# Last attention and expert choice of an eight-phase model: units of two heads and of one head in turn, experts chosen sequence by sequence

## The chip, the core and the metric

The kernel runs on one core of a Trainium2 chip. Its time is the device time in microseconds (us) of one execution. Five engines work side by side, each through its own queue in order: PE (matrix products and transposes), DVE (vector work), ACT (functions such as exp, and copies), POOL (vector work on SBUF, and the indirect DMAs) and SP (which only issues DMAs). They wait for each other through semaphores. "us" is microseconds throughout, and L12 is line 12 of the kernel before unless the text says "after".

## The reference, cut to what matters

Eight sequences of 256 tokens and 256 features pass through four layers; each layer is an attention and a feed-forward block, each followed by a residual and a layer norm. The change touches the last attention and the last block.

```
# last attention, per half sequence of 256 rows (16 heads of width 16, 4 key heads)
scores = softmax(energy / sqrt(D))                # two maps per head, a = 0 and 1
diff   = softmax(where(causal, NEG, scores[0] - lam * scores[1]))
att    = einsum(diff, v); att = att * rsqrt(mean(att * att)) * rms_w * (1 - LAM_INIT)
x      = layernorm(x + att @ Wo)

# last block: 32 experts, the best 4 of each token
p      = softmax(x @ gate)
w, idx = top_k(p, 4); w = w / w.sum()
y[t]   = sum_k w[t, k] * ((u * silu(g)) @ down[idx[t, k]]),   g, u = split(x[t] @ gate_up[idx[t, k]])
x      = layernorm(x + y)
```

The kernel takes whole sequences of 256 tokens, so an attention has 8 sequences, two query blocks of 128 rows each (`qc` 0 and 1; block 0 sees 128 keys, block 1 sees 256) and 16 heads, held as 4 stripes of 32 partitions times 4 heads.

## The kernel before, in words

**Attention, `attn3`.** A *unit* is a query block `qc` and `nh = 2 - qc` heads of each stripe, so that a unit always holds 512 score columns in each of four PSUM banks: two heads with 128 keys, or one head with 256. A sequence has six units. Before the change they run in the order (qc 0, head 0), (qc 0, head 2), then qc 1 with heads 0, 1, 2, 3. The order of all work is written out by hand (a manual schedule for the four compute engines; SP's DMAs are placed by the framework). The loop over `n` (48 units and 3 more turns) does in each turn:

- for the unit before: `factors` (a reciprocal on DVE L671; causal masks L676 and two small products L681, L682 on POOL);
- one step of the queue `others`;
- for unit n: `scores` (32 or 16 matmuls L641, four mask matmuls L654, four maxima on DVE L658, 16 or 8 exponentials on ACT L661);
- for unit n-3: `values` (L738), and a copy of the finished output;
- one step of `projections` (the next sequence's q, k and v: 13 steps, most of them a product L595 and a DVE multiply L599), the first half of `differences` for the unit before (DVE L695 and the maximum L699; POOL L700 and the scaling L703), one or two more steps of `projections` (two when unit n has qc 0);
- one step of `ends` (the finish of an earlier sequence: transposes L755, root mean square, output product L803, residual L164, layer norm, transposes L154; six steps);
- the second half of `differences`;
- two more steps of `others`, unless `self.scattering` is set;
- for unit n-2: `turned` (transposes L720, exponential L722).

DVE, PE, ACT and POOL each carry out their share of that list in exactly this order. The transposes, projections, finish and sort share the PSUM tag `t` with two buffers.

**Sort, `ffn3_sort`, `place`, `tile_experts`, `scatter`.** The tokens are handled in two groups of four sequences (`GROUPS`). For a group the sort computes all gate logits of its eight 128-row pieces (L1906, 32 matmuls with their passes), subtracts the maximum and takes the exponential (L1911 to L1916), finds the best eight and their indices for each piece (L1921, L1922), compares with an iota into one-hot rows (L879), counts and ranks them with matmuls (L893), adds up counts (L896, L898), places every expert at a multiple of 128 rows (L907 to L914), reads out each token's four slots (L921, L922, L926), scatters the rows of X to `rows` in DRAM with 32 indirect DMAs on POOL (L953), finds the expert of each 128-row tile (L935 to L944), and normalises the four weights (L1934 to L1936). It is a generator: the `yield`s cut it in steps. Group 0's sort is put into `others` when sequence 3 is finished, with three scatters a step (`each=3`).

**Experts, `ffn3`, `ffn3_experts`, `ffn3_combine`.** For each group 63 tiles of 128 rows are fetched three at a time (`xg`, L1959, on SP), transposed (L1970, L1972), multiplied by their expert's weights (L1978), passed through silu and a product (L1985, L1987; a one-element POOL copy L1990 follows), transposed back (L1994, L1996), multiplied by the down weights (L2000, L2008) 8 tiles later (4 in group 1) and stored (L2010). The down weights are loaded after the first two fetches, when the attention's buffers come free. During group 0's tiles, `left` is stepped: while more than one generator is left, only at every third tile; it holds the finish of the last sequence, then group 1's sort. During group 1's tiles the outputs of group 0 are gathered (L2045, 32 indirect DMAs on POOL), weighted and normed; group 1's follow at the end.

Of the kernel before, what the change touches and what calls it, by code (L numbers as in the profile page):

```python
# [10 lines left out]
F32 = mybir.dt.float32  # L11
BF16 = mybir.dt.bfloat16  # L12
I32 = mybir.dt.int32
# [26 lines left out]
class Model:  # L40


    def __init__(self, ctx, tc, ins, out):
        self.tc, self.nc, self.ins, self.out = tc, tc.nc, ins, out
        nc = self.nc
        self.const = ctx.enter_context(tc.tile_pool(name="const", bufs=1, side="left"))
        self.small = ctx.enter_context(tc.tile_pool(name="small", bufs=4, side="left"))
        self.psum = ctx.enter_context(
            tc.tile_pool(name="psum", bufs=2, space=bass.MemoryType.PSUM)
        )  # L50
        self.n_ev = 0
        self.rows, self.outs = (
            [
                nc.dram_tensor(f"{x}{g}", (n * P, D), F32, kind="Internal").ap()
                for g, n in enumerate(TILES)
            ]
            for x in ("rows", "outs")
        )
        self.lrows, self.louts = (
            [  # L60
                nc.dram_tensor(f"{x}{g}", (n * P, d), F32, kind="Internal").ap()
                for g, n in enumerate(TILES0)
            ]
            for x, d in (("lrows", ROW0), ("louts", P))
        )
        self.left = []
        self.scattering = False
        self.sorted, self.sorted0 = {}, {}

        c = self.const  # L70
        self.X = [c.tile([P, 2, D], F32, name=f"X{b}", tag=f"X{b}") for b in range(NB)]
        self.xT = [c.tile([P, 2, BLK], F32, name=f"xT{k}", tag=f"xT{k}") for k in range(NBLK)]
        self.ident = c.tile([P, P], F32, name="ident")
        nc.sync.dma_start(out=self.ident, in_=ins["c_ident"])
        self.load_x(0, 2)

        self.tri = c.tile([P, 2 * P], F32, name="tri")
        self.identb = c.tile([P, P], BF16, name="identb")
        nc.vector.tensor_copy(self.identb, self.ident)
        self.maskA = c.tile([P, 4, P], BF16, name="maskA")  # L80
        self.one32 = c.tile([P, 32], F32, name="one32")
        nc.vector.memset(self.one32, 1.0)
        self.nhalf = c.tile([P, 16], F32, name="nhalf")
        nc.gpsimd.memset(self.nhalf, -0.5)
# [25 lines left out]
    def after(self, *call):  # L110

        self.left.append(call)

    def copy(self, out, in_):

# [436 lines left out]
    def attn3(self, w, act, keep, start=False, beside=None):  # L552
# [2 lines left out]

        nc = self.nc
        lam_init = 0.8 - 0.6 * math.exp(-0.3 * 0)

# [187 lines left out]
        def finish(b):  # L748
# [61 lines left out]
            self.normed(b, r, *m)  # L810
            yield
            self.norm_done(b, last=False)
            if beside and b == GROUPS[0][1] - 1:
                others.append(beside(keep))
            yield

        others = []
        projections, ends, done = [], [], []

        def step(queue, n=1):  # L820

            while n and queue:
                if next(queue[0], StopIteration) is StopIteration:
                    queue.pop(0)
                else:
                    n -= 1

        for _ in project(0):
            pass
        units = [  # L830
            Unit(b, qc, h0) for b in range(NB) for qc in range(2) for h0 in range(0, 4, 2 - qc)
        ]
        for n in range(len(units) + 3):

            def at(back):
# [6 lines left out]
                    projections.append(project(u.b + 1))  # L842
            if last:
                last.factors()
            step(others)
            if u:
                u.scores()
            if at(3):
# [5 lines left out]
            step(ends)  # L854
            next(halves, None)
            next(halves, None)
            if not self.scattering:
                step(others, 2)
            if at(2):
                at(2).turned()  # L860
            ends += done
            done.clear()
        return ends + others


    def place(self, w, act, keep, name, idx, n, E=32, tag="t"):
# [1025 lines left out]
            gup=self.load(pool, "f3_gup", [P, 32, 2, 192], split=8),  # L1892
        )

    def ffn3_sort(self, w, g, act, each=1):

        nc = self.nc  # L1900
        first, n = GROUPS[g]
        n *= 2
        lg = self.ps("t")[:, : n * 32].rearrange("p (t e) -> p t e", e=32)
        for t in range(n):
            for c in range(2):
                nc.tensor.matmul(  # L1906
                    lg[:, t, :], self.xt(first + t // 2, t % 2, c), w["gate"][:, c, :],
                    start=(c == 0), stop=(c == 1),
                )
        nm = act.tile([P, n], F32, tag="r_nm", name="r_nm", bufs=1)  # L1910
        nc.vector.tensor_reduce(nm, lg, AX.X, ALU.max)  # L1911
        pr = act.tile([P, n, 32], F32, tag="r_pr", name="r_pr", bufs=1)
        nc.vector.tensor_tensor(
            pr, lg, nm.unsqueeze(2).to_broadcast([P, n, 32]), ALU.subtract
        )
        nc.scalar.activation(pr, pr, AF.Exp)  # L1916
        yield
        top = act.tile([P, n, 8], F32, tag="r_top", name="r_top", bufs=1)
        idx = act.tile([P, n, 8], U32, tag="r_idx", name="r_idx", bufs=1)
        for t in range(n):  # L1920
            nc.vector.max(top[:, t, :], pr[:, t, :])  # L1921
            nc.vector.max_index(idx[:, t, :], top[:, t, :], pr[:, t, :])  # L1922
            if t % 4 == 3 or t == n - 1:
                yield
        one, slots, ends = yield from self.place(w, act, self.const, f"f3{g}", idx[:, :, 0:4], n)
        rows = self.scatter(
            self.rows[g], slots, lambda t, k: self.X[first + t // 2][:, t % 2, :]
        )
        next(rows)
        expert = yield from self.tile_experts(w, act, self.const, f"f3{g}", ends)  # L1930

        wt = self.const.tile([P, n, 4], F32, tag=f"r_w{g}", name="r_w", bufs=1)
        sm = act.tile([P, n], F32, tag="r_sm", name="r_sm", bufs=1)
        nc.vector.tensor_reduce(sm, top[:, :, 0:4], AX.X, ALU.add)  # L1934
        nc.vector.reciprocal(sm, sm)
        nc.vector.tensor_tensor(  # L1936
            wt, top[:, :, 0:4], sm.unsqueeze(2).to_broadcast([P, n, 4]), ALU.mult
        )
        self.sorted[g] = wt, slots, expert
        self.scattering = True  # L1940
        yield
        for i, _ in enumerate(rows):
            if i % each == each - 1:
                yield
        self.scattering = False

    def ffn3_experts(self, w, g, act):


        nc = self.nc  # L1950
        rows, outs, expert, tiles = self.rows[g], self.outs[g], self.sorted[g][2], TILES[g]
        xg, xT, h, hT, er = {}, {}, {}, {}, {}

        def fetch(j):
# [71 lines left out]
                    f(j - i)  # L2026
            yield

    def ffn3_combine(self, g, act, ahead):


        nc = self.nc
        first, n = GROUPS[g]
        wt, slots, _ = self.sorted[g]
        ys, rs = {}, {}
        for t in range(2 * n + ahead):
            i = t - ahead
# [22 lines left out]
                self.norm_done(b)  # L2060
                yield

    def ffn3(self, w, act, left, start=False):

        self.down = None
        if start:
            for b in range(NB):
                self.transpose_x(b)  # L2070
            left = [self.ffn3_sort(w, 0, act)]
        if 0 not in self.sorted:
            for x in left:
                for _ in x:
                    pass
            left = []
        left = list(left) + [self.ffn3_sort(w, 1, act)]
        for j, _ in enumerate(self.ffn3_experts(w, 0, act)):

            if len(left) > 1 and j % 3 != 2:  # L2080
                continue
            while left and next(left[0], StopIteration) is StopIteration:
                left.pop(0)
        for x in left:
            for _ in x:
                pass
        put = self.ffn3_combine(0, act, 2)
        for j, _ in enumerate(self.ffn3_experts(w, 1, act)):

            if j >= 8:  # L2090
                next(put, None)
        for _ in put:
            pass
        for _ in self.ffn3_combine(1, act, 1):
            pass


# [1 line left out]
def tile_layers(ctx: ExitStack, tc: tile.TileContext, ins, out, phases):  # L2099
# [26 lines left out]
    for i, name in enumerate(phases):  # L2126
        m.last = i == len(phases) - 1
        with tc.tile_pool(name=f"act{i}", bufs=2, side=sides[i % 2]) as act:
# [4 lines left out]
            with tc.manual_schedule(engines=engines) if name in MANUAL else ExitStack():  # L2133
# [13 lines left out]
                elif name == "attn1":  # L2147

                    def then(i=i):
                        keeps[i - 1].close()  # L2150
                        open_weights(i + 1)

                    m.attn1(w, act, left, then, start=start)
                elif name == "attn3":
                    beside = None
                    if not m.last:
                        beside = partial(m.ffn3_sort, stack[i + 1][1], 0, each=3)
                    left = m.attn3(w, act, kept[i], start=start, beside=beside)
                elif name == "ffn3":
                    m.ffn3(w, act, left, start=start)  # L2160
                    keeps[i - 1].close()
                else:
                    getattr(m, name)(w, act, start=start)
        stack[i][0].close()
# [125 lines left out]
```

## Time and profile before

| what | us |
|---|---|
| median of 5 runs (lowest to highest) | 2531.3 (2523.01 to 2536.96) |
| the profiled execution | 2531.85 |
| its span in the profile | 2530.1 |
| last attention: first L658 to last L738 | 1767.2 to 2223.9 |
| experts of group 0: first L1970 to last down product L2000 | 2227.85 to 2364.66 |
| experts of group 1: to the last store's landing | to 2473.0 |
| last gathers and norms: to the end | to 2530.1 |

The page gives busy time, not bound time: an engine may be busy for most of a stretch and still not set its length. So the prediction goes by stretches, by what each engine waited for in them, and by the distance between the same instruction of successive units (for attention: the first of the four maxima L658) or tiles (L1987).

### The profile page before, as it was taken

To read this page: it belongs to the slowest core of one execution; us is meant where nothing else is said; L and a number is where in the kernel's file an instruction comes from. 1 tells how busy PE (TensorE), PEld (TensorE's weight loads), DVE (VectorE), ACT (ScalarE), POOL (GpSimd) and SP (SyncE) were. 2 spreads that over 40 slices of the span, in tenths; PEclk is the share of its full clock that TensorE was granted. 3 is DMA by queue.
4 is the path that set the end of the run, shared out by engine and by line. 5 is a ranking of instruction groups with operands and counts; after the bars stand their busy time and mean duration, and the time that the engine had idled before them with its cause. 6 is when DMAs were issued, how large, how long until landed. Compare 5 with 4: busy or idle time off the path is not lost. (4 is left out here: it accounts for less than half of the span.)

```text
span 2530.1 us, 36310 instructions
## 1 busy us (share of the span) xinstructions
PE 2203.4 (87%) x12016; PEld 1493.2 (59%) x12016; DVE 1430.3 (57%) x3593; ACT 1046.9 (41%) x3005; POOL 918.5 (36%) x1725
## 2 busy tenths in 40 slices
PE   7999789899999999999999999998788777678890
PEld 4455588756666666666664465555555554467770
DVE  4555486754544543544465454556888887735363
ACT  1234355553544544544431112221766756634440
POOL 1222443343433323333312320001566657824445
PEclk9999899999999999999999999999989988799995
DMA  5000411100000100000250011002000000155663
GB/s 158 1 1 1 158 46 40 57 9 4 4 3 4 51 1 1 1 1 1 83 195 0 1 50 51 1 1 102 1 2 1 2 1 28 40 144 177 198 195 96
DMA packets 92309, 120.76 MB, mean 48 GB/s; under 512 B 9757, under 2 KB 79582, under 8 KB 91102
## 3 DMA queue, kind: packets, MB, share of 16 engines
q1 hardware_dynamic: 82270, 95.75, 11.7%
q0 software_dynamic: 8192, 21.11, 2.7%
q8 instruction: 100, 1.64, 0.3%
q10 hardware_dynamic: 1664, 1.57, 0.2%
q14 instruction: 83, 0.68, 0.1%
HBM read 67.53 MB, written 50.88 MB: 47 GB/s over the span
## 5 line engine op out<-in xcount | busy, mean ns | idle before, releaser
L1388 POOL TENSOR_SCALAR p<-p,rs 128x128 f32<-128x128 f32 (+1 forms) x256 | 104.8, 429 | 294.4 <-DVE rs L1386 290.1
L1378 ACT ACTIVATE p<-ps_s,nm,rq 128x128 f32<-128x128 f32 (+1 forms) x256 | 128.0, 507 | 151.8 <-DVE nm L1376 151.8
L1306 ACT ACTIVATE sq<-ps_a 128x512 f32<-128x512 f32 x126 | 76.0, 603 | 227.3 <-PE ps_a L1298 225.1
L146 POOL TENSOR_SCALAR rsq<-bnmv 128x2 f32<-128x2 f32 x64 | 13.7, 214 | 383.9 <-DVE bnmv L184 376.3
L661 ACT ACTIVATE e<-ps_a,nm 128x128 f32<-128x128 f32 (+1 forms) x256 | 105.9, 435 | 110.0 <-DVE nm L658 96.4
L1307 DVE TENSOR_REDUCE ssk<-sq 128x4 f32<-128x512 f32 x64 | 43.8, 686 | 172.6 <-ACT sq L1306 172.6
L703 POOL TENSOR_SCALAR v<-e,r,nmd 128x128 f32<-128x128 f32 (+1 forms) x256 | 135.0, 540 | 10.0
L1298 PE MATMUL ps_a<-w_a_wq,xT 128*128 128x512 f32 x256 | 122.3, 600 | 12.1 <-DVE k L1320 9.2
L1978 PE MATMUL ps_a<-w_f_gup,xTg 128*128 x504 | 111.7, 345 | 14.8 <-issue 6.5
L720 PE MATMUL ps_t<-ident,v 128*128 128x128 f32 x384 | 68.2, 314 | 62.1 <-DVE qT L599 30.7
L1298 PE MATMUL ps_a<-w_a_wv,xT 128*128 128x512 f32 x256 | 120.5, 593 | 1.0 <-ACT q L1331 1.0
L695 DVE SCALAR_TENSOR_TENSOR e<-e,c 128x128 f32<-128x128 f32 (+1 forms) x256 | 105.4, 461 | 22.2 <-POOL c L682 22.0
L1307 DVE TENSOR_REDUCE ssq<-sq 128x4 f32<-128x512 f32 x64 | 43.9, 686 | 130.2 <-ACT sq L1306 130.2
L1298 PE MATMUL ps_a<-w_a_wk,xT 128*128 128x512 f32 x248 | 116.5, 593 | 0.0
L1426 PE MATMUL ps_o<-w_a_wo,attT 128*128 128x256 f32 x512 | 111.8, 379 | 0.0
L661 ACT ACTIVATE e<-ps_s,nm 128x128 f32<-128x128 f32 (+1 forms) x256 | 106.8, 452 | 0.0
L1426 PEld LDWEIGHTS ps_o<-w_a_wo,attT 128*128 128x128 f32 x512 | 96.7, 190 | 12.8
L1162 DVE SCALAR_TENSOR_TENSOR yg<-ps_t,xg,yg 128x128 f32<-128x128 f32 x266 | 93.0, 350 | 13.9 <-PE ps_t L1151 3.7
L1365 PE MATMUL ps_s<-kT,qT 128*128 128x256 f32 (+1 forms) x512 | 100.2, 329 | 0.0
L1978 PEld LDWEIGHTS ps_a<-w_f_gup,xTg 128*128 128x128 f32 x504 | 81.8, 196 | 28.6 <-issue 13.8
L720 PEld LDWEIGHTS ps_t<-ident,v 128*128 128x128 f32 x384 | 49.6, 161 | 81.5 <-POOL nmd L700 30.0
L1412 PE MATMUL ps_o<-pT,V 128*128 128x256 f32 x256 | 79.5, 392 | 19.2 <-ACT pT L120 19.2
(410 smaller groups left out, 6067.5 us busy)
## 6 DMA issues: line engine op xcount, KB each, us to landing
rows<-zero SPq DMA_DIRECT2D x42, 384.0 KB
xg<-rows SPq DMA_DIRECT2D x42, 384.0 KB
outs<-yg SPq DMA_DIRECT2D x42, 384.0 KB
w_f_gup<-in_f_gup SPq DMA_DIRECT2D x8, 768.0 KB
w_f_w<-in_f_w SPq DMA_DIRECT2D x8, 512.0 KB
w_f_down<-in_f_down SPq DMA_DIRECT2D x8, 384.0 KB
w_f_up<-in_f_up SPq DMA_DIRECT2D x5, 512.0 KB
lrows<-zero SPq DMA_DIRECT2D x12, 204.0 KB
```

The lines of the kernel that those rows point to most:

```text
L661: nc.scalar.activation(e[:, s, j * nk : (j + 1) * nk], sc[s][:, j, :], AF.Exp, bias=nm[:, s, j : j + 1], scale=1.0, accum_out=sums[:, s, j ...
L695: nc.vector.scalar_tensor_tensor(d[:, s, h, :], u.e[:, s, h, 1, :], u.c[:, s, h : h + 1], d[:, s, h, :], ALU.mult, ALU.add,)
L703: nc.gpsimd.tensor_scalar(u.v[:, s, h, :], d[:, s, h, :], u.r[:, s, h, 0:1], nm[:, s, h : h + 1], ALU.mult, ALU.add,)
L720: nc.tensor.transpose(ps[:, s, c, :], x, self.ident)
L1162: nc.vector.scalar_tensor_tensor(acc[j], y, c, acc[j], ALU.mult, ALU.add)
L1298: nc.tensor.matmul(ps, self.xt(u.b, t, c), w[which][:, c, u.cols], start=(c == 0), stop=(c == 1),)
L1307: nc.vector.tensor_reduce(out, sq, AX.X, ALU.add)
L1365: nc.tensor.matmul(sc[:, j, :], u.qT[:, h0 + j, qc * P : (qc + 1) * P], u.kT[:, h0 + j, 0:nk], start=(j == 0), stop=False,)
L1378: nc.scalar.activation(u.p[qc][:, h0 + j, :], sc[:, j, :], AF.Exp, bias=nm[:, j : j + 1], scale=r[:, j : j + 1], accum_out=u.sums[qc][:, h ...
L1388: nc.gpsimd.tensor_scalar(u.p[qc][:, j, :], u.p[qc][:, j, :], ri[:, j : j + 1], 1.0, ALU.mult, ALU.mult,)
L1426: nc.tensor.matmul(y[:, t, :], attTs[b][:, h, t * P : (t + 1) * P], w["wo"][:, h, :], start=(h == 0), stop=(h == 15),)
L1978: nc.tensor.matmul(ps, xT[j][:, c, :], w["gup"][:, bass.ds(er[j], 1), c, :].rearrange("p o f -> p (o f)"), start=(c == 0), stop=(c == 1),)
```

## The change

Four things change, in `attn3`, `ffn3` and what they call.

- **Order of units.** Within a sequence the units now run (qc 0, head 0), (qc 1, head 0), (qc 1, head 1), (qc 0, head 2), (qc 1, head 2), (qc 1, head 3).
- **Choice by sequence.** `ffn3_sort` is split. `ffn3_choose` does one sequence: logits, a copy out of PSUM, best eight, one-hot rows, counts and ranks; it goes into `others` when that sequence is finished. `ffn3_place` does the rest for a group, once its four sequences are chosen. Sequences 0 to 5 are chosen during the attention; sequence 6 is queued in its last turn and sequence 7 during group 0's tiles, where before all of group 1 was sorted.
- **Scatters have their own queue.** `sends` holds them, two a step for group 0; while it is not empty, the step of `others` ahead of `scores` is a step of `sends`. After the differences `others` has one step, where it had two.
- **The softmax.** The best eight are found on the logits themselves. The exponential of the four best, less the best, and their normalisation are taken per group in `ffn3_weights`: for group 0 ahead of its first tile, for group 1 after its last.

At the start of `ffn3` what is left in `sends` is issued before the first fetch. The core of the diff (`ffn3_place` is the second half of the old sort with other names and other cuts; the counts of a sequence's two pieces are added to those before by one DVE instruction each, and the slots take one more; `step(j)` belongs to `ffn3` and runs once per tile of group 0):

```diff
-            if beside and b == GROUPS[0][1] - 1:
-                others.append(beside(keep))
+            if beside and b < NB - 1:
+                others.append(self.ffn3_choose(beside, keep, b))
+                if b == GROUPS[0][1] - 1:
+                    others.append(self.ffn3_place(beside, 0, keep, sends, each=2))
             yield
...
-            Unit(b, qc, h0) for b in range(NB) for qc in range(2) for h0 in range(0, 4, 2 - qc)
+        order = ((0, 0), (1, 0), (1, 1), (0, 2), (1, 2), (1, 3))
+        units = [Unit(b, qc, h0) for b in range(NB) for qc, h0 in order]
...
-            step(others)
+            step(sends or others)
...
-            if not self.scattering:
-                step(others, 2)
+            step(others)
...
+    def ffn3_choose(self, w, keep, b):
...
+        ps = self.ps("t")[:, :64].rearrange("p (t e) -> p t e", t=2)
+        for t in range(2):
+            for c in range(2):
+                nc.tensor.matmul(ps[:, t, :], self.xt(b, t, c), w["gate"][:, c, :], ...)
+        nc.vector.tensor_copy(lg, ps)
+        yield
+        for t in range(2):
+            nc.vector.max(top[:, t0 + t, :], lg[:, t, :])
+            nc.vector.max_index(idx[:, t, :], top[:, t0 + t, :], lg[:, t, :])
+        nc.vector.tensor_copy(fi, idx[:, :, 0:4])
+        nc.vector.tensor_tensor(one[:, two] ..., ALU.is_equal)
+        yield
+        yield
+        for x, m in ((0, self.ones), (1, self.behind)):
+            for k in range(4):
+                nc.tensor.matmul(ps[:, x], m, one[:, two, k, :], ...)
...
+        yield
...
+    def ffn3_weights(self, g, keep):
+        nc.vector.tensor_tensor(wt, top[:, :, 0:4], top[:, :, 0:1].to_broadcast([P, n, 4]), ALU.subtract)
+        nc.scalar.activation(wt, wt, AF.Exp)
+        nc.vector.tensor_reduce(sm, wt, AX.X, ALU.add)
+        nc.vector.reciprocal(sm, sm)
+        nc.vector.tensor_tensor(wt, wt, sm.unsqueeze(2).to_broadcast([P, n, 4]), ALU.mult)
...
+        def step(j):
+            if ends and j % 3 == 2:
+                self.step(ends)
+                if not ends:
+                    others.append(self.ffn3_choose(w, keep, last))
+                    others.append(self.ffn3_place(w, 1, keep, sends))
+            elif others:
+                self.step(others)
+            else:
+                self.step(sends)
+        wt = self.ffn3_weights(0, keep)
+        while sends:
+            self.step(sends)
```

## The prediction

> **What bounds the kernel now.** The change only touches the last fifth, so I read that by stretches: first the busy time of each engine per stretch, then what DVE waited for in the same stretches, then two stretches of the timeline.
>
> ```profile
> core 0: us, PE busy (x) PEld busy (x) DVE busy (x) ACT busy (x) POOL busy (x), PEclk, DMA share, GB/s
> ...
> 1983.00:2037.00 54.00, 43.21 (x362) 29.82 (x362) 45.95 (x103) 38.15 (x151) 33.62 (x82) 0.91 0.00 1
> 2037.00:2092.00 55.00, 39.42 (x256) 27.18 (x256) 45.06 (x129) 26.93 (x99) 25.85 (x62) 0.75 0.00 1
> 2092.00:2146.00 54.00, 40.68 (x329) 27.25 (x329) 44.44 (x103) 31.77 (x128) 41.04 (x81) 0.88 0.09 33
> 2146.00:2200.00 54.00, 38.30 (x308) 24.92 (x308) 38.04 (x85) 35.78 (x145) 46.12 (x92) 0.78 0.11 40
> ...
> 2244.00:2362.00 118.00, 102.58 (x586) 85.35 (x586) 52.21 (x182) 49.68 (x182) 45.24 (x96) 0.97 0.48 156
> ```
>
> The first row is one undisturbed sequence of the attention: DVE is busy 46 of 54 us, more than any other engine, and PE's waits there are for DVE to empty PSUM. The second holds group 0's sort, the next two its scatters: POOL climbs to 41 and 46. The last row is group 0's experts: PE is busy 103 of 118.
>
> The waits of DVE in the plain stretch, in the sort and in the scatters (who waited, for whom, us in total, times, longest):
>
> ```profile
> DVE V L619 <- PE ps_t L615: 2.7, 1, 2.7
> DVE nm L658 <- PE ps_a L654: 1.9, 2, 1.4
> ...
> DVE r_nm L1911 <- PE ps_t L1906: 3.3, 1, 3.3
> DVE r_upto L896 <- PE ps_t L893: 2.4, 1, 2.4
> ...
> DVE e L695 <- POOL c L682: 7.6, 7, 2.9
> DVE nm L658 <- PE ps_a L654: 7.2, 6, 1.9
> ```
>
> So a plain sequence has some 8 us of DVE waits; the sort adds two waits for its own matmuls; while rows are scattered DVE waits for POOL's factor c. How the scatter stands in POOL's queue:
>
> ```profile
> 2159.62 0.42 POOL L676 TENSOR_SCALAR_AFFINE_SELECT e<-e 128x256 f32<-128x256 f32 x1
> 2160.21 1.03 POOL L953 DMA_INDIRECT rows<-X,r_slots  x1 [0.17 <-issue]
> 2161.54 0.97 POOL L953 DMA_INDIRECT rows<-X,r_slots  x1 [0.30 <-issue]
> 2162.82 0.96 POOL L953 DMA_INDIRECT rows<-X,r_slots  x1 [0.30 <-issue]
> 2163.81 0.29 POOL L700 TENSOR_TENSOR nmd<-nmd,r 128x2 f32<-128x2 f32 x1
> ...
> 1932.95 0.20 POOL L700 TENSOR_TENSOR nmd<-nmd,r 128x4 f32<-128x4 f32 x1 [1.47 <-DVE nmd L699]
> ```
>
> Three scatters of 1.28 us stand between the masks and L700, and L700 then starts at once: POOL was late. Without scatters (last line) POOL waits at that place for DVE.
>
> **The change part by part.** The sum is made against the profiled execution, 2531.85 us (span 2530.1 and 1.75 around it); the median of the runs is 2531.3, so a difference holds for both.
>
> *The old sort leaves the attention.* From one unit's first L658 to the next, in the timeline: units 32 to 36, with the sort, took 15.17, 15.61, 13.07, 9.49 and 10.73, together 64.1; the same places a sequence earlier (26 to 30) 9.63, 8.22, 7.06, 9.88 and 10.20, together 45.0. **-19.1**. The sort's own DVE instructions sum to 14.5 in the groups of that stretch: DVE work is paid here nearly one for one, plus 4.6 of waits.
>
> *Six choices come in, per sequence.* DVE, each: copy of 128x64 logits, between L896's 0.19 and the 128x128 copy's 0.29: 0.23; per piece L1921 and L1922 are 0.39 apart from the next: 0.8; cast 0.17; one-hot row of 256 elements 0.42 (L914's size); counts and slot 3 x 0.2. Together 2.25. PE: 8 passes of L1906's 0.11 (3.5 us for 32) and 8 of L893 (0.9 at four times the width). The copy stands behind the second half of the differences, when its matmuls have long been possible; but PE's first maxima of the next unit already come 1.9, 1.5 and 1.4 us late at this place of a sequence (L658's wait of units 15, 21 and 27), and the best-eight instructions, 1.4 us, fill that wait. Against it, the logits hold one of the two buffers of `t`, so that the two transposes of `turned` go one after the other (one exponential of 0.6 between them). Counts and ranks stand ahead of the next scores on PE: 0.3 to 0.9. From below: 1.4 of 2.25 hidden and little of PE's part left, 1.0 each. From above: the two waits of the old sort stay at full size, 3.3 + 2.4 + 2.25 = 7.9 each. The old 3.3 was for 32 passes and the new one for 8 that are issued early, so I go by the DVE work: 2.0 each, **+12** (6 to 47).
>
> *Placement stays*, in smaller steps: L907 to L926 ran from 2081.92 to 2087.5 without a gap, the experts of tiles 1.3: **+6.9** (6 to 8.5). Weights, 0.6, go to the start of the experts, where everything waits for DMA.
>
> *Scatters, two a unit in place of three.* POOL's wait ahead of L700 in a plain sequence (1874 to 1928) was 1.47, 1.74, 3.36, 1.81, 1.48 and 2.32. Three scatters, 3.84, overflow it by 1.8 on average; two, 2.56, by 0.67. Units 37 to 41 took 48.97 against 43.33 for 25 to 29; units 42 to 46 took 44.53 against 43.6, though the projections of a next sequence were missing, 13 x 0.41, of which 4.5 fall to five units. So 11 units paid about 11 for an overflow of 20; 15 units with an overflow of 10 pay 5.5. **-5.5** (-10 to 0).
>
> The clock belongs here. In the scatter stretches TensorE was granted 0.88 and 0.78, in the plain one 0.91, and the sort's row has 0.75. [...] I stay with POOL's count, since the plain row falls below full clock as well.
>
> *Order of units.* Nothing is added or removed: per sequence DVE's sum is the same 46. POOL's longer share of a two-head unit (masks 1.28 against 0.84, scaling 3.5 against 2.2) no longer comes twice running, where DVE waited 0.4 for c (unit 14); but the second one now meets the finish's square roots, where POOL waits 1.95 for ACT's tables, and c was late by 1.2 (unit 17) already. **0** (-5 to +5).
>
> *Start of the experts.* Before, the scatters ended at 2211.2, and the first fetch, waiting for the attention's last buffers, went out at 2224.08; six tiles were done by 2239 and the seventh waited for its rows until 2244.4, behind 3.1 MB of down weights at some 240 GB/s. After the change the last four scatters stand behind POOL's last scaling (2222.1), 5.1 us, and land about 2229.5. SP is in order: two of the eight weight loads go ahead of the fetch, the other six queue behind it. The bytes are the same; the DMA engines lose the gap, about 1.5 to 2, and PE restarts without the 5.7 us pause. **+1.5** (0 to 6).
>
> *Group 0's tiles.* L1987's 21st to 30th starts took 27.3 us, the next 23 1.67 each: the old sort cost 10.6 there (logits 3.5 and two table loads of 1.28 in one tile of 7.12, counts 3.0, the rest under 1 a tile). After the change it is one sequence's choice, no table load, and the same placement: 0.8 + 0.5 + 0.9 + 2.1 = 4.3. **-6.3** (-9 to -2). The last scatter of group 1 comes after the 63rd tile's product in place of the 62nd, and the fetch behind it, with two stores behind that on SP, was the last wait at this boundary (PE idle 3.7 before 2363.9): **+1.4** (0 to 2).
>
> *Group 1's weights* need a table load (1.28) after the last silu. Eight gathers of 1.25 on POOL come first in time: 0; without this cover 2.5.
>
> Sum: -19.1 + 12 + 6.9 - 5.5 + 0 + 1.5 - 6.3 + 1.4 = **-9.1**: 2522.7, given as 2523.
>
> **The rivals.**
>
> *More is hidden.* 8 us of DVE waits per sequence stand open. If the choices fall into them down to the lower end (1.0 each, -6) and the order of units takes 4 with it: -19, **2512.5**. For it: the score waits of units 15, 21 and 27 stand exactly where the best-eight instructions come. Against: the old sort paid more than its DVE work.
>
> *Slower: each choice waits on PE.* Place: the logits' copy and the counts, each an in-order DVE instruction behind a fresh matmul, with the next maxima, the exponentials and the projections queued behind it. Price: half of the old waits, 2.9 and 2.25, 5.2 each. The gain is gone from 3.5 each on; above 4.8 the kernel is slower by more than 0.3%. At 5.2: +19 on the sum, **2542**.
>
> *It does nothing measurable.* If the attention goes by DVE's sum alone, sort and choices together are 6 x 2.25 + 6.9 - 14.5 = +5.9 (in place of -0.2), and if the first tiles wait for the late scatters at the upper end, +6: 5.9 - 5.5 + 6 - 6.3 + 1.4 = +1.5, **2533**. For it: the first row above, and the place of the last scatters. Against: the five long units, which lost more than the sort's own instructions.
>
> **How the numbers follow.** Forecast 0.45, more hidden 0.17, nothing measurable 0.18, slower 0.20. Measurement tells about 0.3%, 7.6 us, from no change: faster is below 2524.3. The forecast's own range is -16 to -2 (2516 to 2530), of which 0.28 is faster, 0.17 the same. Faster 0.28 + 0.17 = 0.45, with 0.01 of the third case 0.46; same 0.17 + 0.17 = 0.34; slower 0.20. The range runs from the second case with the scatters' lower end (-23.5, 2508) to the slower case at its named price, 2542; below and above about 0.1 each.
>
> **What would show it.** The five units with the sort shrink from 64 to about 53; each sequence with a choice grows from 54.4 by about 2; DVE's wait for c falls from 7.6 to about 3 in a stretch of 100 us; no L1911-like wait above 1 us at the choice's copy; the first fetch goes out 4 to 6 us after the last attention product, the seventh tile's rows land about 22 us after it; the 21st to 30th tile products take about 21 us. I am wrong if the choices' DVE waits exceed 1.5 each, if the order of units moves a plain sequence by over 1 us, or if the seventh tile comes later than 26 us after the attention.

## The result and the profile after

The changed kernel takes 2538.0 us (median; 2527.7 to 2541.7) against 2531.5 of the kernel before on the same chips: a ratio of 1.0021, 95% interval 1.0014 to 1.0027. The forecast was 2523 us; the time lies in its range, on the other side of no change and within the 0.3% named there. The profiled execution took 2538.62 us (span 2536.9).

Lines have moved: L658 is now L667 (maxima of the scores), L695 and L699 are L704 and L708, L700 and L703 are L709 and L712, L682 is L691, L720 is L729, L953 is L956. From the first maximum of unit 0 to that of unit 46 the attention took 427.1 us before and 436.5 after. Busy time by stretch after the change, with the columns that the prediction's first fence has: three sequences with a choice each (units 12 to 29), the scatters (units 36 to 45) and group 0's tiles.

```profile
1866.10:2044.10 178.00, 134.79 (x1140) 90.96 (x1139) 141.39 (x342) 111.58 (x439) 101.84 (x246) 0.90 0.00 1
2106.10:2205.60 99.50, 74.11 (x581) 50.70 (x581) 77.24 (x189) 61.16 (x252) 75.45 (x151) 0.81 0.09 30
2244.00:2362.00 118.00, 103.87 (x601) 87.18 (x601) 54.30 (x181) 52.21 (x188) 45.28 (x104) 0.94 0.59 183
```

Units 12 to 29 took 160.7 before with 136.55 of DVE work. Now they take 17.3 more, and DVE only 4.8 more of work: the loss is waits. What DVE waited for in units 36 to 45, after:

```profile
DVE nm L667 <- PE ps_a L663: 13.0, 4, 4.0
DVE e L704 <- POOL c L691: 3.6, 3, 2.3
```

As forecast, the wait for POOL's factor c fell, from 7.6 to 3.6. But the wait for PE's scores grew from 7.2 (9.0 with those put down to the other PSUM tag) to 13.0, and the ten units took 99.5 against 97.5.

In what follows a sequence's six turns are numbered first to sixth, a *plain* sequence is one without sort, choice or scatters, and the *pair* is the second unit of two heads, (qc 0, head 2): second in its sequence before, fourth after the change. Kernels ran in sessions in which the kernel before took 2523.3 to 2532.8; so ratios to it are given.

### The profile page after: what moved, and what is told of

It reads as the page before. It is cut to its first block, busy times and chain, and to the rows that moved or that the text cites. A ratio compares the mean times of both kernels' runs of the same rounds, so it can differ in the third digit from the quotient of the medians.

```text
span 2536.9 us, 36429 instructions
## 1 busy us (share of the span) xinstructions
PE 2210.7 (87%) x12064; PEld 1496.2 (59%) x12064; DVE 1430.5 (56%) x3617; ACT 1045.1 (41%) x3004; POOL 920.8 (36%) x1723
## 5 line engine op out<-in xcount | busy, mean ns | idle before, releaser
L712 POOL TENSOR_SCALAR v<-e,r,nmd 128x128 f32<-128x128 f32 (+1 forms) x256 | 138.3, 552 | 10.1 <-POOL nmd L709 0.2
L729 PE MATMUL ps_t<-ident,v 128*128 128x128 f32 x384 | 72.3, 323 | 60.8 <-ACT p L731 21.0
L704 DVE SCALAR_TENSOR_TENSOR e<-e,c 128x128 f32<-128x128 f32 (+1 forms) x256 | 101.4, 446 | 22.4 <-POOL c L691 22.2
L1165 DVE SCALAR_TENSOR_TENSOR yg<-ps_t,xg,yg 128x128 f32<-128x128 f32 x266 | 93.0, 350 | 13.8 <-PE ps_t L1154 3.5
L1368 PE MATMUL ps_s<-kT,qT 128*128 128x256 f32 (+1 forms) x512 | 99.5, 327 | 0.0
L729 PEld LDWEIGHTS ps_t<-ident,v 128*128 128x128 f32 x384 | 50.5, 165 | 82.3 <-POOL nmd L709 22.4
L2059 PEld LDWEIGHTS ps_a<-w_f_gup,xTg 128*128 128x128 f32 x504 | 82.6, 198 | 25.9 <-issue 11.7
L1415 PE MATMUL ps_o<-pT,V 128*128 128x256 f32 x256 | 79.5, 392 | 19.2 <-ACT pT L128 19.2
```

Of the source, the lines that this page charges most:

```text
L704: nc.vector.scalar_tensor_tensor(d[:, s, h, :], u.e[:, s, h, 1, :], u.c[:, s, h : h + 1], d[:, s, h, :], ALU.mult, ALU.add,)
L712: nc.gpsimd.tensor_scalar(u.v[:, s, h, :], d[:, s, h, :], u.r[:, s, h, 0:1], nm[:, s, h : h + 1], ALU.mult, ALU.add,)
L729: nc.tensor.transpose(ps[:, s, c, :], x, self.ident)
L1165: nc.vector.scalar_tensor_tensor(acc[j], y, c, acc[j], ALU.mult, ALU.add)
L1368: nc.tensor.matmul(sc[:, j, :], u.qT[:, h0 + j, qc * P : (qc + 1) * P], u.kT[:, h0 + j, 0:nk], start=(j == 0), stop=False,)
L2059: nc.tensor.matmul(ps, xT[j][:, c, :], w["gup"][:, bass.ds(er[j], 1), c, :].rearrange("p o f -> p (o f)"), start=(c == 0), stop=(c == 1),)
```

## The experiments

### The order alone, and everything but the order

`e1_order_only` and `e8_order_only_again` (one execution more, with a profile) are the kernel before with the new order:

```
-            Unit(b, qc, h0) for b in range(NB) for qc in range(2) for h0 in range(0, 4, 2 - qc)
+        order = ((0, 0), (1, 0), (1, 1), (0, 2), (1, 2), (1, 3))
```

> The kernel before, with nothing but the new order of units. Theory A (each choice is dear: it stalls PE and DVE for more than its own instructions; the order is neutral): 2532 us, within 1.5 of the kernel before, since the first sequences without a choice grew by only 0.5 each. Theory B (the order of units costs the time, through PSUM of two outputs held at once and the longer turns that follow each other): 2538 to 2541, about +1 a sequence or more.

> The kernel before with only the new order, a second profile: the first one showed the attention no longer than before (427.3 us from its first maximum to unit 46, against 427.2) though the kernel took 5 us more. If that was one execution's luck of the clock, the attention is 430 to 434 here, and time again near 2537; if the loss lies in front of the attention, the first maximum is again near 1772 us and the attention near 427.

`e2_old_order` is the changed kernel with `order = ((0, 0), (0, 2), (1, 0), (1, 1), (1, 2), (1, 3))`.

> The changed kernel with the old order of units. Theory A: 2538 us, as the changed kernel; a sequence with a choice still grows by 4 to 7 us. Theory B: 2530 to 2532, the order's cost goes away. Where the two act together (a choice falls badly only beside the new order), it lies below the changed kernel although the order alone costs nothing.

Measured: `e1_order_only` 2537.7 us, 1.0020 (1.0011 to 1.0030); `e8_order_only_again` 2539.6, its attention 432.2 where the first profile had 427.2; `e2_old_order` 2526.1, **0.9979 (0.9969 to 0.9990)**. So Theory B holds in its main point: the order costs 5.0 us alone and 0.42%, 10.6 us, in the changed kernel, and all else in the change is a gain of 0.21%. That the choices also grow their sequences by 4 (Theory A) is true as well, see below, but it is less than they save. Theory B's reason, two outputs held in PSUM at once, is not what the waits show: all that PE waits for ahead of the products into `ps_o` are exponentials p, 12.5 us in the whole attention before and 12.9 and 15.0 in the two profiles of the order alone.

The end of a plain sequence changes visibly. First the kernel before, then `e1_order_only`, in the timeline, at the same place (fifth and sixth turn of sequence 4):

```profile
2011.60 1.34 POOL L703 TENSOR_SCALAR v<-e,r,nmd 128x256 f32<-128x256 f32 x2
2015.24 0.25 POOL L781 TENSOR_TENSOR ms<-ms,rr 128x32 f32<-128x32 f32 x1 [1.95 <-ACT rr L780]
...
2018.01 1.10 POOL L703 TENSOR_SCALAR v<-e,r,nmd 128x256 f32<-128x256 f32 x2
...
2019.98 1.00 DVE L695 SCALAR_TENSOR_TENSOR e<-e,c 128x256 f32<-128x256 f32 x2 [0.65 <-POOL c L682]
```

```profile
2017.24 2.03 POOL L703 TENSOR_SCALAR v<-e,r,nmd 128x128 f32<-128x128 f32 x4
2021.53 0.25 POOL L781 TENSOR_TENSOR ms<-ms,rr 128x32 f32<-128x32 f32 x1 [1.95 <-ACT rr L780]
...
2024.32 1.76 POOL L703 TENSOR_SCALAR v<-e,r,nmd 128x128 f32<-128x128 f32 x4
...
2026.94 1.00 DVE L695 SCALAR_TENSOR_TENSOR e<-e,c 128x256 f32<-128x256 f32 x2 [2.53 <-POOL c L682]
```

The finish's square roots (L781, waiting 1.95 for ACT) stand on POOL between the two halves of a unit's scaling L703. Four instructions of one head make 2.4 us, eight of two heads 3.8. With the pair in fourth place its scaling lies there; c for the next unit, and with it DVE, comes 2.5 late in place of 0.65. Over three plain sequences this wait is 1.23 in the mean before, 1.88 and 2.17 in the two profiles of the order alone; the sixth turn is 9.7 before, 10.4 and 10.5 with the new order. Eight times 0.75 would be 6, about the 5 measured. That this wait is the price is not shown, and two things speak against it: in `e1_order_only` the attention as a whole is no longer than before, because third turns are shorter (8.0 in the mean in place of 9.6), and the place of the pair that turns out to be free, below, has the same wait.

### How far a stage of one profile stands

`e15_before_again` is the kernel before, unchanged.

> The kernel before itself, a second profile: if its attention (from the first maximum to unit 46) is again within 1 us of 427.2, the order's cost in the attention is what two profiles of the order alone showed (0.1 and 5.0); if it comes to 423 to 425, stages of single profiles differ by as much as the effects, and only the medians and the means over like turns count.

2538.4 us in this one execution. Its attention is 427.2 (427.1 before), but its first maximum came at 1771.4 us in place of 1767.2, and group 0's tiles took 2.4 more. So 4 us of difference ahead of the attention, the 1772 of `e1_order_only` too, mean nothing. The attention of the kernel before repeats itself; that of the order alone, one program as well, does not: 427.2 and 432.2. Turns with the same work differ there together with the granted clock. The first turn of sequence 3, in `e1_order_only` and then in `e8_order_only_again`:

```profile
1923.58:1933.73 10.15, 8.86 (x73) 6.04 (x72) 8.22 (x20) 7.37 (x35) 5.75 (x14) 1.00 0.00 0
1921.14:1932.97 11.83, 9.52 (x64) 6.68 (x62) 8.23 (x20) 7.38 (x35) 5.73 (x14) 0.86 0.01 1
```

DVE, ACT and POOL do the same work to 0.02 us; at a clock of 0.86 the turn takes 1.7 more. The third turns of sequences 3 and 4 took 7.7 and 7.9 at 0.99 and 0.91, and 9.2 and 9.3 at 0.81 and 0.82. So the cost of the order is shown by the medians; which turns bear it, two profiles (0.1 and 5.0) can't tell, and a difference of 5 us between single profiles of an attention proves nothing.

Tiles differ by session, a set of runs taken together. From group 0's 46th tile to its 63rd, five profiles from the two sessions in which the kernel before took 2523 to 2524 have 25.2 to 26.1 us, whatever the kernel (`e9`, `e10`, `e11`, `e12`, `e16`); all 13 others have 29.5 to 32.7. Group 1's tiles took 93.4 to 95.5 there and 97.7 to 102.1 elsewhere. That is about the difference between the sessions; its cause is open.

### The place of the pair

```
e9   order = ((0, 0), (1, 0), (0, 2), (1, 1), (1, 2), (1, 3))
e10  order = ((0, 0), (1, 0), (1, 1), (1, 2), (0, 2), (1, 3))
```

Both are the kernel before otherwise. `e12_finish_later` has the change's order, one `yield` more ahead of the finish's square roots, and its last one dropped.

> The kernel before with the second unit of two heads third in its sequence (after one unit of one head), in place of second (before) or fourth (the change's order, 2537.7 and 2539.6). Theory C (the order costs because the scaling of that unit's two heads on POOL, 3.8 us against 2.4, stands around the finish's chain of square roots in the fifth turn, so that the next factor c and DVE come late): its scaling now lies a turn ahead of that chain, 2530 to 2534. Theory D (any order in which units of two heads are apart costs, by PE's idle stretches and the clock): 2535 to 2539.

> The kernel before with the second unit of two heads fifth in its sequence. Theory C: its scaling lies a turn behind the chain of square roots, 2530 to 2535. Theory D: 2535 to 2540.

> The kernel before with the change's order of units, and the finish's square roots (and all behind them) one turn later, so that they meet a unit of one head. Theory C: most of the 5 us come back, 2531 to 2535; the wait for c in the last turn of a sequence falls from some 2 to 1.2 or less. Theory D: 2536 to 2540.

Third place: 0.9993 (0.9984 to 1.0001). Fourth: 1.0020. Fifth: **1.0030 (1.0020 to 1.0040)**. Theory D falls: units may alternate at no cost. Theory C in its narrow form, that only the turn of the square roots is dear, falls with the fifth place: there the sixth turn is still 10.7 and the first of the next sequence 11.2 to 12.5 (10.2 before). What stands is that the pair is free in the first half of its sequence and dear in the half in which the finish of the sequence before is under way. Sixth turn and next first turn together (means over sequences 2 to 4) go the same way: 19.9 before, 19.2 with the pair third, 20.8 and 21.5 fourth, 22.4 fifth. The wait for c does not: in `e9_pair_at_2`, which costs nothing, the sixth turn of sequence 4 has

```profile
2021.64 1.01 DVE L695 SCALAR_TENSOR_TENSOR e<-e,c 128x256 f32<-128x256 f32 x2 [1.88 <-POOL c L682]
```

and the mean of three is 1.85, as in `e1_order_only` (1.88); with the pair fifth, the dearest place, it is 1.55. So the place decides, but by which wait is open. `e12_finish_later` came to 1.0016 (1.0007 to 1.0024): the wait for c falls to 0.23 and the time does not come back. Its sixth turns are 7.0 in place of 10.5, its first ones 12.0 to 13.0, and its attention 424.0 against 427.2 and 432.2; but the sort starts a turn later too and the last scatter comes 24.6 after unit 46 instead of 18.6. As a whole it decides nothing.

`e13_after_pair_at_2` is the changed kernel with the order of e9:

> The changed kernel, with the second unit of two heads third in its sequence in place of fourth: units still alternate between one unit of two heads and one or more of one head. Theory C (what costs is that unit's nearness to the finish): as with the old order, 0.997 to 0.999 of the kernel before. Rival (the choices cost more beside any alternation): 1.001 or more.

0.9970 (0.9959 to 0.9980), attention 423.8 against 436.5. Moving this one unit by one place in each sequence turns the changed kernel from a loss into a gain, choices and all.

### What a choice costs

`e3_three_choices_late` leaves the choices of sequences 4 to 6 to group 0's tiles:

```
-            if beside and b < NB - 1:
+            if beside and b < GROUPS[0][1]:
...
+        for b in range(GROUPS[1][0], last):
+            others.append(self.ffn3_choose(w, keep, b))
```

> The changed kernel, but sequences 4 to 6 make their choice among group 0's expert tiles, as the last one does. Theory A: three choices of about 5 leave the attention and come back at 1 to 2 each in the tiles, 2526 to 2530 us. Theory B: the choices are about 2 each, as forecast, and the tiles take them for nearly as much: 2535 to 2539.

2534.1 us, 1.0008 (1.0000 to 1.0017): between the two, nearer to B. Units 36 to 45 took 91.6 in place of 99.5, some 4 a choice for two; the sixth tile came 60.1 after unit 46 in place of 56.8, and the tiles took 102.2 in place of 99.6. But the profiled execution, 2526.6, was the fastest of its twelve, so its stages are rather too short. In sequences 2 to 4 the mean of the three profiles with the changed kernel's units (178.0, 177.3 in `e4_three_scatters`, 172.7 here) stands 12.5 over the mean of the two with the order alone (161.2, 165.7), 4.2 a choice; with the old order it is 172.0 against 160.7, 3.8 (4.4 by `e7_old_order_late_choices` below, with the same units, 173.9). So a choice costs about 4 under either order, where 2.0 was forecast and DVE's own part is 2.25.

Where the other 2 go: the logits' matmuls L1924 in the changed kernel between 1860 and 2205 us, by source line.

```profile
L1924 PE MATMUL ps_t<-w_f_gate,xT x48: 267/297/422, 1890.6 to 2192.5; 128*128 128x32 f32 x48
its engine sat idle before it (us, times) until:
  ACT xT L128: 6.2, 3
  DVE xT L126: 4.0, 2
```

PE sat idle 10.2 us ahead of five of six choices, 2.0 each, until the copy of the transposed rows xT was done, which the finish's last step had only just asked for. Behind the logits stand the unit's transposes, and behind these the next scores. In the timeline of the changed kernel (third turn of sequence 4):

```profile
2007.76 0.68 DVE L126 COPY xT<-ps_t 128x512 f32<-128x512 f32 x1
...
2008.49 1.91 PE L1924 MATMUL ps_t<-w_f_gate,xT 128*128 128x32 f32 x8 [2.22 <-DVE xT L126]
...
2012.15 1.09 PE L729 MATMUL ps_t<-ident,v 128*128 128x128 f32 x4 [0.84 <-ACT p L731]
...
2015.84 0.69 DVE L667 TENSOR_REDUCE nm<-ps_a 128x4 f32<-128x512 f32 x1 [3.55 <-PE ps_a L663]
```

2.22 for xT, then 0.84 more for the second transpose, which needs the PSUM buffer that the logits took; DVE, its best-eight work long done, waits 3.55 for the scores, where it waited 1.4 before.

`e5_choice_behind_turned` puts the matmuls behind the transposes and DVE's part a step later, in the changed kernel; `e6_old_order_mended` does so with the old order and three scatters, `e11_mended_attention_only` likewise but not among the tiles:

```
-            step(others)
             if at(2):
                 at(2).turned()
+            step(others)
...
-        nc.vector.tensor_copy(lg, ps)
         yield
+        nc.vector.tensor_copy(lg, ps)
...
-        yield
...
                     start=(x == 0 and k == 0), stop=(x == 1 and k == 3),
                 )
+        yield
```

> The changed kernel with each choice's matmuls issued behind the unit's transposes of its differences and its DVE work one step later, so that no transpose waits for a PSUM buffer that the logits hold and DVE never stands at fresh logits or counts. Theory A (a choice of about 5 us is 2.3 of DVE work and the rest PE's late scores behind its matmuls): five choices save 2 to 2.5 each, 2525 to 2529. Theory B (the time is DVE's own work and the lower clock that the choice's turns bring, wherever the matmuls stand): 2536 to 2539.

> The old order of units, three scatters a unit, and the choices issued as in e5_choice_behind_turned. If the three parts add up with what was measured (old order -12 against the changed kernel, three scatters -6) and Theory A of e5_choice_behind_turned holds (-10): 2512. If the choices' place brings nothing: 2520. If three scatters only helped by the new order's idle time: 2526.

> As e6_old_order_mended, but the choice among the expert tiles issued as in the changed kernel (there the logits held a PSUM buffer one tile longer, and one tile took 1.25 us more). 1 to 1.5 us less than e6_old_order_mended: 2523 to 2524; if that wait is hidden by the weights' transfer, 2525.

In the attention Theory A holds: sequences 2 to 4 take 171.4 in `e5_choice_behind_turned` (172.7 to 178.0 without), 167.8 in `e6_old_order_mended` and 167.9 in `e11_mended_attention_only` (172.0 and 173.9 without), which is 2.4 a choice under the old order, and there DVE's wait for scores behind a choice (units 15, 21, 27) falls from between 2.7 and 3.3 to 0.4 at most. The kernels gained little: 1.0015 (1.0007 to 1.0024), 0.9967 (0.9956 to 0.9977) and 0.9964 (0.9952 to 0.9976). One reason shows in `e11_mended_attention_only`, in the fifth turn of sequence 6, which takes 13.8 in place of 9 (who waited, for whom, us in total, times, longest):

```profile
PE ps_t L729 <- ACT p L731: 4.9, 1, 4.9
```

While rows are scattered, scatters take the choice's step ahead of the scores; its logits then hold a PSUM buffer for a whole turn, and PE waits 4.9 between two transposes, for an exponential that stands on ACT behind the finish's square roots (L788 and L789, 2136.2 to 2140.8). `e16_both_step` steps both:

```
-            step(sends or others)
+            step(sends)
+            step(others)
```

> e11_mended_attention_only, with scatters and a choice both stepped ahead of the scores, so that no choice's logits hold a PSUM buffer through a turn while rows are scattered. If that buffer is what the turn of 13.8 us waits for: that turn falls to some 9, and the kernel to 0.994 to 0.9955 of the kernel before (e11: 0.9964). If POOL's scatters are the cause: as e11.

That turn falls to 6.8, the attention to 417.8, and the kernel to **0.9944 (0.9929 to 0.9959)**, 2507.3 against 2523.3: faster than the kernel before and the changed one, though its interval still overlaps that of `e11_mended_attention_only`. Not all of the attention's 6.7 is this step's: 4.2 lie ahead of unit 36, where both kernels issue the same work in the same order. From unit 36 to the last product it is 127.4 in place of 131.8: the turn's 7 came back by more than half in its neighbours (the sixth turn 11.3 in place of 7.4, the third 12.7 in place of 11.1), but a wait of 6.2 ahead of the counts in the turn of unit 46 is gone too. Its logits wait 0.5 us in all:

```profile
L1925 PE MATMUL ps_t<-w_f_gate,xT x48: 232/276/420, 1888.4 to 2171.6; 128*128 128x32 f32 x48
its engine sat idle before it (us, times) until:
  ACT p L731: 0.5, 2
```

`e14_mended_pair_at_2` is e11 with the pair in third place.

> e11_mended_attention_only with the second unit of two heads third in its sequence. By Theory C the place is free: 0.996 of the kernel before, as e11. If the shorter sequences that e9_pair_at_2 showed (its attention 423.6 us against 427.2) are no luck: 0.994 to 0.995.

0.9990 (0.9981 to 0.9999): neither. Its attention is no longer (424.0), though it has a turn of 15.3 of the same kind. Group 0's tiles took 104.8 against 102.1 in `e13_after_pair_at_2` of the same session, with the same work in them; that is hardly more than two profiles of the kernel before differ by (2.4). Why it is slower is open.

### Scatters and the start of the experts

`e4_three_scatters` is the changed kernel with `each=3`. `e7_old_order_late_choices` joins it with the old order and the late choices.

> The changed kernel with three scatters of rows in a unit in place of two. If two a unit save what was forecast (5.5 us in the attention): 2540 to 2543. If the scatters fall on POOL's idle time anyway and their late end delays the start of the experts by 4 us: 2534 to 2536.

> The old order of units, three scatters a unit, and the choices of sequences 4 to 6 among group 0's expert tiles (the others as in the changed kernel). Measured alone: old order -12, three scatters -6, late choices -4. If they add up: 2516. If the old order makes a choice cheap enough in the attention that the tiles charge as much: 2520 to 2523.

`e4_three_scatters`: 2532.1 us, 1.0004 (0.9994 to 1.0015), some 4 us (0.17%) better than two a unit. In units 36 to 45 it takes 100.6 against 99.5; but its scatters end 4.8 after unit 46, not 33.5, and the sixth tile comes 54.1 after unit 46, not 56.8. After the change, POOL and SP in the timeline:

```profile
2238.15 0.96 POOL L956 DMA_INDIRECT rows<-X,r_slots  x1 [0.31 <-issue]
```

```profile
2236.76 0.82 SPq L140 DMA_DIRECT2D w_f_down<-in_f_down  x2
2242.75 0.92 SPq L2040 DMA_DIRECT2D xg<-rows  x2
2243.71 3.70 SPq L140 DMA_DIRECT2D w_f_down<-in_f_down  x6
```

The last scatter ends at 2239.1, and the first fetch goes out when it has landed (4.46 from the start of its issue, at 2242.6), 6.1 after the last attention product's end at 2236.6; six of eight weight loads stand behind it. `e7_old_order_late_choices`: 0.9980 (0.9970 to 0.9989). The parts don't add up: on top of the old order, late choices and three scatters are worth nothing. By the profiles the attention is no shorter (427.2 against 425.6 in `e2_old_order`), and the tiles charge 4 us (103.4 against 99.3) for what the start of the experts saves (51.1 from unit 46 to the sixth tile, against 56.5).

## Why the prediction failed, step by step

Forecast beside measurement, all but the order (`e2_old_order` against the first profile before; the second, `e15_before_again`, has 51.5 and 111.3 where the table has 53.1 and 108.9):

| Step | forecast | measured |
|---|---|---|
| three choices, units 12 to 29 | 3 x 2.0 = +6 | 172.0 - 160.7 = +11.3 |
| units 30 to 35: old sort out, choice and placement in | -19.1 + 2.0 + 6.9 = -10.2 | 60.1 - 73.1 = -13.0 |
| units 36 to 45: two choices, two scatters a unit | +4 - 5.5 = -1.5 | 98.5 - 97.5 = +1.0 |
| start of the experts, unit 46 to sixth tile | +1.5 | 56.5 - 53.1 = +3.4 |
| group 0's tiles, with the last choice | -6.3 | 99.3 - 108.9 = -9.6 |
| boundary of the groups | +1.4 | 11.7 - 11.3 = +0.4 |
| sum | -9.1 | -6.5 (by the medians' ratio: -5.3) |

- **Order of units, "0 (-5 to +5)": the step that failed.** It cost 5.0 alone and 10.6 in the changed kernel, twice the upper end. The working looked at the right place (the pair meets the finish) and set it at nothing because DVE's work is the same. What the runs showed in its place: with the same work the pair is free in third place, costs 0.20% in fourth and 0.30% in fifth. The late c that the working named is not the price (1.85 in the free order). Its own sign, a plain sequence longer by over 1 us, stayed undecided: 0.2 and 1.6 in two profiles. Without this step the sign of the forecast would have been right.
- **Choices, 2.0 each: a mis-sized term, about 4.** The sentence "its matmuls have long been possible" was false: xT was written just ahead of them, and PE waited 2.0 a choice. The prediction looked for the wait at DVE's copy, where it was small as forecast (0.6 at most); the slower rival, "each choice waits on PE", had the engine right and 4 of its 5.2, but by itself, without the order, this did not make the kernel slower.
- **Old sort and placement: better than forecast** by 3, the tiles too (20th to 30th 18.5 against 27.3; 21 was forecast). The five long units shrank from 64 to 53.4 as named.
- **Scatters, -5.5.** As a whole two a unit lost some 4 us against three (`e4_three_scatters`): 1.1 gained in units 36 to 45, more lost behind them by the late end. POOL's time was freed (DVE's wait for its c: 7.6 before, 3.6 after) and DVE then waited for the scores instead (7.2 before, 13.0 after). Without choices beside them the term may be right: 91.6 in `e3_three_choices_late`, a fast execution, against 96.8 and 96.6 with the order alone, some 5, close to POOL's count; the granted clock was 0.84 before and 0.87 there.
- **Start of the experts, +1.5: measured 3.4 to 3.7.** The path was right (scatters behind POOL's last scaling, SP in order); the first fetch went out 6.1 after the last product, at the upper edge of the 4 to 6 named. The rows for the seventh tile were in time, 22.3 after.

Open stays by which wait the order costs, and why twice as much beside the choices (0.42% against 0.20%; the two intervals leave 0.06 to 0.38% for the difference). In `e5_choice_behind_turned` the attention is 12 us shorter than in the changed kernel; 3 of it went between the first fetch and the sixth tile and 4 in the tiles (103.6 against 99.6), for reasons that are open too.

## What to carry to other kernels

Reordering units with equal sums of work need not be free (0.20% here), and the wait that a trace shows late at the new place need not be the price: try the places one by one, by medians, before trusting a cause. Two profiles of one program differed by 5 us here (427.2 and 432.2), with the clock low at different turns, so compare the same turns with their clock beside them. When a step is put "as soon as its input is done", look up who writes that input and when: here PE's wait of 2.0 a choice held up the transposes and scores behind it, and behind the transposes it fell to 0.5 for all choices together (`e16_both_step`). A PSUM buffer held across a scheduling step that something else can take over can become a stall, as in the turn of 13.8 us with its wait of 4.9.

## What the runs showed of the hardware

The same turn of the same units (first of sequence 4) took 12.2 us in the changed kernel and 10.8 in `e3_three_choices_late`; the granted clock was 0.86 there and 0.98 here. Short stretches of the first (busy time by engine, then the clock):

```profile
1984.00:1986.00 2.00, 0.22 (x2) 0.00 (x0) 2.00 (x5) 2.00 (x14) 1.30 (x5) 1.00 0.01 4
1986.00:1988.00 2.00, 1.28 (x5) 0.83 (x5) 1.97 (x5) 2.00 (x13) 0.35 (x2) 0.85 0.00 0
1988.00:1990.00 2.00, 2.00 (x5) 1.63 (x6) 0.13 (x1) 1.03 (x6) 1.63 (x3) 0.50 0.01 4
```

PE was idle for 1.8 us, worked for 1.1, fell idle again at 1987.1 for 0.7, and was granted half clock from 1987.4 to 1990.8, just when DVE waited for its product (3.2 in place of 1.75 for the residual L172). The five profiles with the change's units (`e1`, `e8`, the changed kernel, `e3`, `e4`) have twenty such first turns in sequences 2 to 5: sixteen took 10.1 to 10.8 at a clock of 0.98 or more, four took 11.8 to 12.2 at 0.86. The 28 of the seven profiles with the old order took 10.1 to 10.5 at 0.97 or more. So these spells may be a part of what the order costs; no run tests that. The half-clock spell is 3.4 long; in the 3.4 us before the drop PE was idle for 1.8 and 0.3 with work between, and the turn took 1.4 more.
